# Moving the queries' second task one place ahead, and the first image's sums between its weight copies

## The chip, the core and the metric

The kernel runs on one core of a Trainium2 chip. The core has a matrix engine (TensorE, "PE"; its weight loads have a row of their own, "PEld"), an elementwise engine (VectorE, "DVE"), an engine for functions and copies (ScalarE, "ACT"), GpSimd ("POOL") and a queue that issues transfers ("SP"). Each engine works through its own list of instructions in order and waits at semaphores for the others. The metric is the device time in microseconds (us), as the median of several runs. One more run is recorded by the hardware profiler: that is the profile and the trace.

## The reference

Two layers of attention work on an image batch x of 8 x 32 x 32 x 256, in fp32. An image is N = 1024 rows of C = 256 values.

```
layer 0:  q, k, v = x W_qkv        4 heads, each 256 wide
          a = softmax(q k^T / 16)  over all 1024 rows of the image
          x1 = concat(a v) W_out + b_out + x
layer 1:  f = x1 Wf + bf;  g = x1 Wg + bg       32 wide
          h = x1 Wh + bh                        256 wide
          out = gamma * softmax(g f^T) h + x1
```

## The kernel before

**Folded weights.** Each head's matrices are folded once: wqk from the query and key weights, wvo from the value and output weights. Scores then need one projection of x (the "queries" q) against x itself, and the attention sums x rows directly, followed by one product with wvo. `fold_weights(h)` (L281) makes five tasks: three turns (transposes of the query, key and value weights on TensorE, each with a copy out of the accumulation memory) and two multiplications with their copies. `copy_on` puts copies on VectorE and ScalarE in turn. After wqk is copied, four sums of its quarters are made on VectorE (wt).

**Seven products instead of eight.** Layer 0's large products are cut in 2 x 2 blocks and done with seven block products (`seven`, L222). They need sums of blocks of both factors, made on VectorE: xs of the keys (`key_sums`, L346), xt of the values (`value_sums`, L362), qs of the queries and s/ss of the probabilities. A call of `seven` gives three tasks. It holds three banks of accumulation memory, x, y and z, throughout:

```
one:    x <- product 1, y <- 6, z <- 5;  e = copy of x (ScalarE);  u = y + e (VectorE)
two:    x <- x + 2, y <- y + 7;          11 = x (ScalarE);  v = y + e;  22 = z + v (VectorE)
three:  y <- y + 4, z <- z + 3;          21 = y + e;  12 = z + u (VectorE)
```

So TensorE's product 7 waits until u is made, and product 4 until v is made, since both add to a bank that VectorE reads. The instructions of all these tasks stand at one line of the profile, L235 for the matmuls and L252 for the additions, and are told apart by the tiles: psx_q, psy_q, psz_q, u_q, v_q belong to the queries, psx, psy, psz, u, v to scores, psx_y and so on to the products with the values. The pool "ps" has six banks and "psm" two; layer 1's scores (ps_l) and products (pa_l) take single banks of "ps", turns, folds and projections (po) those of "psm" (L762).

**Stages.** A unit is a head of layer 0 or an image's layer 1; a step is one half (blk 0 or 1, 512 columns) of a unit. An image's four heads are followed by the next image's; layer 1 of image b-1 stands behind the second head of image b (for the last image behind the fourth). The order on TensorE, VectorE and ScalarE is written out by hand: in each step i the tasks are put at places, numbers from about 0 to 10, and run in their order (`put`, L809). A step does the scores of its own unit, the sums and products of the step before (`one`), the rest of the products and the projection with wvo of the step before that (`two`), and in blk 1, if the next unit is a head, that head's queries (L841) and their sums qsums (L842). These are the places that a layer-0 step gives:

```
scores             0, 2, 4, 6, 8, 10     (two calls of seven, three tasks each)
products of two    1 (third task);  inverse 2.9;  projection 3 and 7
sums of one        2.2, 3.2, 4.2, 5.2;  products of one 5, 9
queries            1.5, 3.5, 4.5;  value_sums (h = 0, blk = 1, b > 0) 1.4, 2.4, 3.4, 4.4
```

A layer-1 step in blk 1 has its two tasks of four score matmuls (ps_l, each on 32 rows of the array, each followed by a copy to s_l on ScalarE) at 0.5 and 2, its softmax pieces from 0.9 to 7.5, the products of its first half (pa_l) at 1, 4, 6, 8, the projection at 3 and 7, and the queries at 2.5, 4.5 and 6.5.

**Start.** Ahead of step 0 come the transposes of the first image (px), the fold of head 0, the key sums, the first queries and their sums, the scaling of bh by gamma and the first image's value sums (L789 to L793). Step 0 then has the folds of heads 1 to 3, fifteen tasks at 0.3, 0.9, 1.5 and so on (L837).

Of the kernel before, what the change touches and what calls it, by code (L numbers as in the profile page):

```python
# [12 lines left out]
ALU = mybir.AluOpType  # L13
# [7 lines left out]
def kernel(  # L21
# [51 lines left out]
    nc = tc.nc  # L73
# [39 lines left out]
    rows, rows1 = {}, {}  # L113
# [36 lines left out]
    bh_sb = const.tile([P, C], F32, tag="bh", name="bh_sb")  # L150
    gamma_sb = const.tile([P, 1], F32, tag="gamma", name="gamma_sb")
# [129 lines left out]
    def fold_weights(h):  # L281

        wT, hold = [], []
        folded[h] = []

        def turn(i, what):
            w, _ = weights[h]
            pt = tile_of("psm", [P, NB], f"pw{what}_{h}")
            for d in range(CC):
                for c in range(CC):  # L290
                    nc.tensor.transpose(
                        pt[:, d * C + c * P : d * C + (c + 1) * P],
                        w[:, c, i * C + d * P : i * C + (d + 1) * P],
                        ident,
                    )
            if i != 1:
                hold.append(tile_of("y", [P, N], f"w{what}T_{h}"))
            t = hold[-1][:, ts(i % 2, NB)]
            copy_on(i, t, pt)
            wT.append(t.rearrange("p (d c) -> p d c", d=CC))  # L300

        def multiply(i, what):
            wqT, wkT, wvT = wT
            pm = tile_of("psm", [P, NB], f"p{what}_{h}")
            for c in range(CC):
                for d in range(CC):
                    nc.tensor.matmul(
                        pm[:, ts(c, C)],
                        lhsT=(wqT, wvT)[i][:, d, ts(c, P)],
                        rhs=wkT[:, d, :] if i == 0 else weights[h][1][:, d, :],  # L310
                        start=(d == 0),
                        stop=(d == CC - 1),
                    )
            t = const.tile([P, CC, C], F32, tag=f"{what}{h}", name=f"{what}{h}")
            copy_on(i, t.rearrange("p c e -> p (c e)"), pm)
            folded[h].append(t)
            if i == 0:
                t4 = const.tile([P, 4, P], F32, tag=f"wt{h}", name=f"wt{h}")
                sums = [t4[:, k, :] for k in range(4)]
                blocks = [t[:, c, ts(e, P)] for c in range(CC) for e in range(CC)]  # L320
                run(sum_b(sums, *blocks))
                wblocks[h] = b_operands(blocks, sums)

        tasks = [partial(turn, i, what) for i, what in enumerate(("q", "k", "v"))]
        tasks += [partial(multiply, i, what) for i, what in enumerate(("wqk", "wvo"))]
        return tasks


    xT_of, x1T_of, xblocks, vblocks = {}, {}, {}, {}

    def transpose_rows(b, src, dst, layer):


        def task(k, c):
            if b not in dst:
                dst[b] = tile_of("xT", [P, CC, N], f"x{layer}T_{b}")
            pt = tile_of("psm", [P, NB], f"px{layer}_{b}_{k}_{c}")
            for t in range(HT):
                nc.tensor.transpose(
                    pt[:, ts(t, P)], src[b][:, k * HT + t, ts(c, P)], ident  # L340
                )
            nc.scalar.copy(dst[b][:, c, ts(k, NB)], pt)

        return [partial(task, k, c) for k in range(NBLK) for c in range(CC)]

    def key_sums(b):  # L346

        made = {}

        def piece(i):  # L350
            if i == 0:
                xT = xT_of[b]
                t = tile_of("v", [P, 4, HN], f"xs_{b}")
                sums = [t[:, k, :] for k in range(4)]
                blocks = [xT[:, c, ts(k, HN)] for k in range(2) for c in range(CC)]
                made["l"] = sum_a(sums, *blocks)
                xblocks[b] = a_operands(blocks, sums)
            made["l"][i]()

        return [partial(piece, i) for i in range(4)]  # L360

    def value_sums(b):  # L362

        made = {}

        def piece(i):
            if i == 0:
                r = rows[b]
                t = tile_of("xt", [P, 4, NT // 2, P], f"xt_{b}")
                blocks = [r[:, ts(j, NT // 2), ts(c, P)] for j in range(2) for c in range(CC)]  # L370
                sums = [t[:, k] for k in range(4)]
                made["l"] = sum_b(sums, *blocks)
                vblocks[b] = b_operands(blocks, sums)
            made["l"][i]()

        return [partial(piece, i) for i in range(4)]
# [368 lines left out]
    def run(*lists):  # L745
        for l in lists:
            for t in l:
                t()
# [39 lines left out]

    first = steps[0][0]  # L789
    queries, qsums = first.queries()  # L790
    run(transpose_rows(0, rows, xT_of, 0), fold_weights(0), key_sums(0), queries, qsums)
    nc.vector.tensor_scalar(bh_sb, bh_sb, gamma_sb, None, ALU.mult)
    run(value_sums(0))  # L793

    def is_l0(s):
        return s is not None and isinstance(s[0], Layer0)
# [7 lines left out]
    for i, (a, blk) in enumerate(steps):  # L804
        l0 = isinstance(a, Layer0)
        one, two, nxt = step(i - 1), step(i - 2), step(i + 1)
        places = []

        def put(tasks, *at):  # L809
            assert len(tasks) == len(at)  # L810
            places.extend(zip(at, range(len(places), len(places) + len(at)), tasks))

        if l0:
            put(a.scores(blk), 0, 2, 4, 6, 8, 10)
        else:
            tasks, pieces = a.scores(blk)
            put(tasks, *((0.5, 2.4) if blk == 0 else (0.5, 2)))
            put(pieces, *((1.6, 3.9, 6.2, 6.5, 7.4, 8.4, 8.6) if blk == 0 else
                          (0.9, 2.7, 4.2, 5, 6.2, 6.8, 7.5)))
        if is_l0(two):  # L820
            u, k = two
            put(u.products_of[k][2:], 1 if l0 else 0)
            put([partial(u.invert, k)], 2.9 if l0 or blk == 1 else 1.9)
            put(u.project(k), *((3, 7) if l0 else (2, 6) if blk == 0 else (3, 7)))
        if is_l0(one):
            u, k = one
            sums, keys = u.sums(k)
            u.products_of[k] = u.products(k)
            put(sums[:2] + sums[3:], *((2.2, 3.2, 4.2) if l0 else (0.8, 2.2, 4.5)))
            put(sums[2:3], 5.2 if l0 else 5.5)  # L830
            put(keys, *((6.2, 8.2) if l0 else (7.6, 9.6)))
            put(u.products_of[k][:2], *((5, 9) if l0 else (4, 7)))
        elif one is not None:
            put(one[0].products(one[1]), *((3, 5, 7, 9) if l0 else (1, 4, 6, 8)))
        if i == 0:
            fold = fold_weights(1) + fold_weights(2) + fold_weights(3)
            put(fold, *[0.3 + 0.6 * n for n in range(len(fold))])  # L837

        if is_l0(nxt) and blk == NBLK - 1:
            queries, qsums = nxt[0].queries()  # L840
            put(queries, *((1.5, 3.5, 4.5) if l0 else (2.5, 4.5, 6.5)))  # L841
            put(qsums, *((5.4, 6.4, 7.2, 7.4) if l0 else (6.7, 6.9, 7.3, 7.6)))  # L842

        if l0 and a.h == 0 and blk == 0:
            put(residual(a.b), 5.3, 6.3, 7.3, 7.4)
        if l0 and a.h == 0 and blk == 1 and a.b > 0:
            put(value_sums(a.b), 1.4, 2.4, 3.4, 4.4)
        if l0 and a.h == 2 and blk == 0 and a.b + 1 < B:
            load_x(a.b + 1)
        if l0 and a.h == HEADS - 1 and blk == 0 and a.b + 1 < B:  # L850
            put(transpose_rows(a.b + 1, rows, xT_of, 0), 1.5, 2.5, 3.5, 4.5)
            put(key_sums(a.b + 1), 5.4, 6.4, 7.2, 7.4)

        if l0 and a.b > 0 and a.h == behind(a.b) - 1:
            if blk == 0:
                put(transpose_rows(a.b - 1, rows1, x1T_of, 1), 2.5, 4.5, 6.5, 8.5)
            else:
                put(nxt[0].queries(), 1.4, 1.5, 3.5)
        if not l0 and blk == 0:
            put(a.values(), 0.9, 1, 3, 5, 8)  # L860
        if nxt is None:
            put(transpose_rows(B - 1, rows1, x1T_of, 1), 8.1, 8.2, 8.3, 8.4)
            put(final.queries(), 9, 9.1, 9.3)
        for _, _, t in sorted(places, key=lambda x: x[:2]):
            t()
# [82 lines left out]
    with tc.If(bad > 0), ExitStack() as general:  # L948
# [5 lines left out]
        for b in range(B):  # L954
# [3 lines left out]
            for h in range(HEADS):  # L958
                a = General0(b, h)
# [4 lines left out]
            a = Layer1(b)  # L964
# [37 lines left out]
```

## Time and profile before

The time is 2407.64 us, the median of 3 runs (2407.25 to 2407.84). The profiled execution has a span of 2406.9 us.

| engine | busy us | share |
|---|---|---|
| TensorE, matmul | 2367.2 | 98% |
| TensorE, weight load | 1946.1 | 81% |
| VectorE | 1585.7 | 66% |
| ScalarE | 623.8 | 26% |
| GpSimd | 236.5 | 10% |

A row of the trace in order of time gives the start in us, how long it took, the engine, the line in the code, the operation, written tile<-read tiles, shapes and the number of instructions merged; brackets show how long the engine stood idle before it and whom it waited for. A row of the list of waits gives the waiting engine with the tile it wanted to write, the engine and tile that released it, and the total time, the number of times and the longest. Matmuls overlap a little: a row's duration is longer than the distance to the next row's start, and it is that distance which adds up to the span. A row of the view by stages gives the stage, its length, the busy time of each engine (with the number of instructions), the granted share of TensorE's clock, the share of the transfer engines and GB/s.

### The profile page before, as it was taken

What the parts mean: (1) busy time and instruction counts of PE and PEld (TensorE: products, weight loads), DVE (VectorE), ACT (ScalarE), POOL (GpSimd) and SP (SyncE); (2) the same over time, 40 slices, a digit from 0 to 9 for tenths busy, and PEclk for the clock granted to TensorE, in tenths of its full rate; (3) what the DMA queues carried; (4) which work ended last, traced back from release to release, by engine and by line L of the source; (5) the groups of instructions that cost most, each with busy time, mean ns of one, the idle gap of its engine ahead of it and who ended that gap; (6) DMA issues with size and microseconds to landing.
All of it is one profiled execution on the core that took longest, in us unless ns stands there. A gap on an engine that the chain in (4) does not pass through costs nothing.

```text
span 2406.9 us, 25909 instructions
## 1 busy us (share of the span) xinstructions
PE 2367.2 (98%) x10608; PEld 1946.1 (81%) x10608; DVE 1585.7 (66%) x2477; ACT 623.8 (26%) x1001; POOL 236.5 (10%) x93
## 2 busy tenths in 40 slices
PE   8999999999999999999999999999999999999999
PEld 6888888788887888778887788878888788888877
DVE  5666666567675666766667567675676756766665
ACT  2222222222232222322123222232222322222232
POOL 0111101011110111101111011110111100011110
PEclk9999999999999999999999999999999999999999
DMA  3000000000000000000000000000000000000000
GB/s 116 1 1 1 1 18 1 18 1 1 18 1 18 1 18 1 1 18 1 18 1 1 18 1 18 1 1 18 1 18 1 1 18 1 1 1 1 1 10 28
DMA packets 43535, 23.63 MB, mean 10 GB/s; under 512 B 36048, under 2 KB 38096, under 8 KB 43408
## 3 DMA queue, kind: packets, MB, share of 16 engines
q1 hardware_dynamic: 43408, 21.90, 3.2%
q8 instruction: 85, 1.39, 0.2%
q14 instruction: 42, 0.34, 0.0%
HBM read 13.37 MB, written 8.52 MB: 9 GB/s over the span
## 4 chain that ended last, share of the span: by engine, by line
PE 91%; DVE 8%; issue 0%; DMA 0%; ACT 0%; SPq 0%; DVEq 0%
PE psy_y L235 13%; PE psy L235 13%; PE pa_l L730 9%; PE psx_y L235 9%; PE psx L235 9%; PE psz_y L235 9%; PE psz L235 8%; PE po L586 8%; PE psy_q L235 3%; PE psz_q L235 2%; PE pr_v_l L419 2%; PE psx_q L235 1%; DVE s L529 1%; DVE ss L529 1%; PE pm_fg L399 1%; PE ps_l L651 1%
## 5 line engine op out<-in xcount | busy, mean ns | idle before, releaser
L542 POOL PARTITION_ALL_REDUCE rb<-rs x64 | 206.9, 3233 | 1942.2 <-DVE rs L540 1942.2
L235 PE MATMUL psy<-qs,xs 128*128 128x256 f32 x1024 | 262.9, 379 | 2.2 <-DVE qs L461 2.2
L235 PE MATMUL psz<-q,xs 128*128 128x256 f32 x1024 | 263.2, 380 | 0.0
L235 PE MATMUL psx<-q,x0T 128*128 128x256 f32 x1024 | 262.8, 379 | 0.0
L490 ACT ACTIVATE p<-p 128x1024 f32<-128x1024 f32 x128 | 135.4, 1058 | 456.9 <-DVE p L252 456.9
L586 PE MATMUL po<-wvo,y 128*128 128x256 f32 x1024 | 242.1, 379 | 0.0
L235 PE MATMUL psx_y<-p,x 128*128 128x256 f32 x1024 | 241.9, 379 | 0.0
L235 PE MATMUL psy_y<-s,xt 128*128 128x256 f32 x1024 | 241.9, 379 | 0.0
L730 PE MATMUL pa_l<-v_l,s_l 128*128 128x257 f32 x1024 | 231.7, 381 | 2.3 <-DVE y L252 1.9
L235 PEld LDWEIGHTS psx<-q,x0T 128*128 128x128 f32 x1024 | 193.9, 190 | 40.1 <-issue 15.8
L730 PEld LDWEIGHTS pa_l<-v_l,s_l 128*128 128x128 f32 x1024 | 193.7, 190 | 39.0 <-issue 12.7
L235 PEld LDWEIGHTS psx_y<-p,x 128*128 128x128 f32 x1024 | 192.9, 190 | 36.0 <-issue 12.0
L586 PEld LDWEIGHTS po<-wvo,y 128*128 128x128 f32 x1024 | 192.8, 190 | 31.2 <-issue 6.5
L235 PEld LDWEIGHTS psy<-qs,xs 128*128 128x128 f32 x1024 | 194.5, 190 | 29.0 <-DVE qs L461 2.6
L235 PEld LDWEIGHTS psz<-q,xs 128*128 128x128 f32 x1024 | 194.7, 190 | 26.5
L235 PEld LDWEIGHTS psy_y<-s,xt 128*128 128x128 f32 x1024 | 193.7, 190 | 27.3
L252 DVE TENSOR_TENSOR u<-psy,e 128x512 f32<-128x512 f32 x128 | 88.5, 692 | 164.3 <-PE psy L235 91.6
L264 ACT ACTIVATE p<-psx 128x512 f32<-128x512 f32 x128 | 76.4, 597 | 373.5 <-PE psx L235 373.4
L252 DVE TENSOR_TENSOR v<-psy,e 128x512 f32<-128x512 f32 x128 | 88.2, 689 | 115.1 <-PE psy L235 114.9
L235 PE MATMUL psy<-qs,x0T 128*128 128x256 f32 x512 | 131.4, 379 | 0.0
L258 ACT COPY e<-psx 128x512 f32<-128x512 f32 x128 | 73.9, 577 | 217.8 <-PE psx L235 217.8
L597 DVE SCALAR_TENSOR_TENSOR x<-po,inverse,x 128x256 f32<-128x256 f32 x256 | 112.0, 479 | 25.4 <-PE po L586 15.6
(108 smaller groups left out, 3152.6 us busy)
## 6 DMA issues: line engine op xcount, KB each, us to landing
out_dram<-x SPq DMA_DIRECT2D x15, 512.0 KB, 2.6
x<-in_x_dram SPq DMA_DIRECT2D x14, 512.0 KB, 4.6
w<-in_L_conv_W_qkv_dram SPq DMA_DIRECT2D x4, 768.0 KB
x<-in_x_dram SPq DMA_DIRECT2D x4, 256.0 KB, 4.7
w<-in_L_conv_W_out_dram SPq DMA_DIRECT2D x4, 256.0 KB, 9.8
line<-rb SPq DMA_DIRECT2D x64, 2.0 KB
st<-line SPq DMA_DIRECT2D x64, 2.0 KB, 2.1
out_dram<-x SPq DMA_DIRECT2D x4, 128.0 KB, 2.1
```

Of the source, the lines that this page charges most:

```text
L235: nc.tensor.matmul(banks[k][:, ts(i, w)], lhsT=lhsT, rhs=rhs, start=first and n == 0, stop=True, skip_group_check=True,)
L252: nc.vector.tensor_tensor(dst, shaped(banks[k]), shaped(other), ALU.add)
L258: nc.scalar.copy(scratch("e"), banks["x"])
L264: copy(outs["11"](), shaped(banks["x"]))
L399: nc.tensor.matmul(pm[:m], lhsT=w()[:, c, d * P : d * P + m], rhs=src()[:, c, ts(k, NB)], start=(c == 0), stop=(c == CC - 1),)
L419: nc.tensor.matmul(pm[:, ts(j, C)], lhsT=src()[:, c, ts(2 * t2 + j, P)], rhs=w()[:, c, :], start=(c == 0), stop=(c == CC - 1),)
L490: exp(both, both)
L529: made["l"][i]()
L542: nc.gpsimd.partition_all_reduce(t, r.rearrange("p e i -> p (e i)"), P, bass_isa.ReduceOp.add)
L586: nc.tensor.matmul(pm[:, ts(j, C)], lhsT=self.y[blk][:, c, ts(2 * t2 + j, P)], rhs=folded[self.h][1][:, c, :], start=(c == 0), stop=(c == ...
L597: nc.vector.scalar_tensor_tensor(acc, pm[:, ts(j, C)], inverse[:, n : n + 1], acc, ALU.mult, ALU.add)
L730: nc.tensor.matmul(pm[:, : C + 1], lhsT=p[:, j, ts(ti, P)], rhs=v[:, j, : C + 1], start=(j == 0), stop=(j == NT - 1),)
```

## The change

The queries' second task goes one place ahead, so that the projection and the scores' third task stand between it and the queries' third task. After a layer-1 unit and in step 1, where there is no projection, the first task goes ahead as well; inside a layer-1 unit all three do. At the start, three of the four key sums go between the copies of the folded weights, two turns of head 1 go ahead of the first scores, the other folds are spaced anew, and the first image's value sums and the scaling of bh move into step 1.

```
 queries, qsums = first.queries()
-run(transpose_rows(0, rows, xT_of, 0), fold_weights(0), key_sums(0), queries, qsums)
-nc.vector.tensor_scalar(bh_sb, bh_sb, gamma_sb, None, ALU.mult)
-run(value_sums(0))
+turn_q, turn_k, turn_v, *multiply = fold_weights(0)
+sums = key_sums(0)
+run(transpose_rows(0, rows, xT_of, 0), [turn_q, turn_k, sums[0], turn_v], sums[1:3])
+run(multiply, sums[3:], queries, qsums)
...
     fold = fold_weights(1) + fold_weights(2) + fold_weights(3)
-    put(fold, *[0.3 + 0.6 * n for n in range(len(fold))])
+    put(fold, -2, -1, *[0.9 + 0.6 * n for n in range(len(fold) - 2)])
+if i == 1:
+    put([partial(nc.vector.tensor_scalar, bh_sb, bh_sb, gamma_sb, None, ALU.mult)], 8.5)

 if is_l0(nxt) and blk == NBLK - 1:
     queries, qsums = nxt[0].queries()
-    put(queries, *((1.5, 3.5, 4.5) if l0 else (2.5, 4.5, 6.5)))
+    put(queries, *((1.5, 2.5, 4.5) if not l0 or is_l0(two) else (0.5, 1.5, 4.5)))
...
-if l0 and a.h == 0 and blk == 1 and a.b > 0:
+if l0 and a.h == 0 and blk == 1:
     put(value_sums(a.b), 1.4, 2.4, 3.4, 4.4)
```

## The prediction, made before the result was known

> **What bounds the kernel now.** I read the page first, then the list of waits, then TensorE's instructions in order of time around each gap. The page, busy time by engine:
>
> ```profile
> PE 2367.2 (98%) x10608; PEld 1946.1 (81%) x10608; DVE 1585.7 (66%) x2477; ACT 623.8 (26%) x1001; POOL 236.5 (10%) x93
> ```
>
> TensorE is busy 98% of 2406.9 us, so only what lies between its matmuls (39.7 us) can be won without removing matmuls, and the change removes none. The waits of TensorE name what ends those gaps (total us, times, longest):
>
> ```profile
> PE psy_q L235 <- DVE v_q L252: 21.5, 26, 1.5
> PE psy L235 <- DVE qs L461: 2.2, 1, 2.2
> PE psy_q L235 <- DVE xs L358: 0.7, 1, 0.7
> PE pwv L291 <- ACT wqT L172: 0.7, 1, 0.7
> ```
>
> The first is the third task of the queries waiting for VectorE's v_q, which must read bank y before TensorE adds to it. In order of time its 26 cases fall into three sizes plus the first, 0.78 at 22.56: 7 of 1.47 (steps with h=0, blk=1, b>0), 7 of 1.06 (i=1, and the L0 steps right after an L1 unit) and 11 of 0.27. One of the large ones:
>
> ```profile
> 607.00 1.02 PE L235 MATMUL psx_q<-x0T,wqk 128*128 128x512 f32 x2
> 607.86 1.02 PE L235 MATMUL psy_q<-xs,wt 128*128 128x512 f32 x2
> ...
> 608.81 0.88 DVE L597 SCALAR_TENSOR_TENSOR x<-po,inverse,x 128x256 f32<-128x256 f32 x2
> 609.58 1.03 PE L235 MATMUL psz<-q,xs 128*128 128x256 f32 x4
> 609.60 1.22 DVE L529 TENSOR_TENSOR s<-ss,p 128x1024 f32<-128x1024 f32 x1
> 610.74 0.69 DVE L374 TENSOR_TENSOR xt<-x,xt 128x512 f32<-128x512 f32 x1
> 611.34 0.69 DVE L252 TENSOR_TENSOR v_q<-psy_q,e_q 128x512 f32<-128x512 f32 x1
> 612.08 1.12 PE L235 MATMUL psy_q<-x0T,wt 128*128 128x512 f32 x2 [1.48 <-DVE v_q L252]
> 613.04 1.02 PE L235 MATMUL psz_q<-xs,wqk 128*128 128x512 f32 x2
> ```
>
> psy_q was done at 608.7, but v_q stands on VectorE behind two products, a sum and a value sum. Start to start a pair of matmuls takes 0.86; from 609.58 to 613.04 there should be 1.72 and are 3.46, so such a case costs 1.74. The same count gives 0.54 for a small case (126.80 to 129.06) and 1.32 for one after L1 (485.16 to 488.20). The six queries inside L1 units wait for nothing.
>
> At the start TensorE idles from 25.4 to 27.57, and its clock then falls to half:
>
> ```profile
> 25.60:28.90 3.30, 1.32 (x6) 1.20 (x7) 3.20 (x6) 0.43 (x1) 0.00 (x0) 1.00 0.34 138
> 28.90:32.40 3.50, 2.83 (x12) 2.11 (x10) 3.39 (x6) 0.58 (x1) 0.00 (x0) 0.51 0.00 0
> ```
>
> (The column before the last two is the granted clock, the third TensorE's busy time.)
>
> [...] four ps_l matmuls on 32 rows take 1.07 together (428.70 to 429.77). [...] The kernel gives 6 to "ps" and 2 to "psm", so a seventh live "ps" tile waits.
>
> **The change part by part.** I worked the times out by hand from the order and waits of the changed program and durations of these rows.
>
> *L0 steps behind an L0 unit, 18 cases.* The second task moves from behind the projection to ahead of it. TensorE then has two.queries, projection (1.72), three of scores (1.72), three.queries; VectorE has v_q before inverse, x and the second sum. In the case above: one.queries and two of scores end at 605.27 as before, two.queries at 606.99 (u_q done 603.65, no wait), projection to 608.71, scores to 610.44. VectorE: v 605.47, p, ss to 608.0, value sum to 608.6, v_q 608.6 to 609.2, the next add 609.9, both ahead of 610.44. No wait. VectorE then runs on without a gap: second sum to 612.2, value sum to 612.9; psy_y needs both and would start at 613.90. So 1.0 us of slack, and the whole 1.74 is kept: 7 x 1.74 = 12.2. The 11 small ones have 2.2 us of slack at the same place: 11 x 0.54 = 5.9.
>
> *L0 steps after an L1 unit and i=1, 7 cases.* Without a projection nothing lies between the tasks: the order is one.queries, two.queries, two of scores, three of scores, three.queries. The wait changes its tile: three of scores now follows two of scores at once and waits for v. Nearest row: the first queries, whose tasks also touch (20.75, 22.56, 23.52: 2.77 for 1.72, so 1.05 lost). 1.32 - 1.05 = 0.27, x 7 = 1.9 saved. In i=1 the first image's value sums (4 x 0.68 on VectorE) come in too; psy_y needs the third about 0.8 after it is there, so nothing.
>
> *L0 queries inside an L1 unit, 6 cases: a new wait.* Today all four ps_l of the second score task come before one.queries. Moved to 1.5 the queries hold three of six banks (x, y, z stay live until their third task) and ps_l gets three; in the changed program the fourth waits for ScalarE's copy of the first of the four. Rows:
>
> ```profile
> 428.70 1.14 PE L651 MATMUL ps_l<-fg 32*128 32x512 f32 x8
> 429.77 1.12 PE L235 MATMUL psx_q<-x0T,wqk 128*128 128x512 f32 x2
> 429.85 2.06 ACT L660 COPY s_l<-ps_l 128x512 f32<-128x512 f32 x4 [3.00 <-PE ps_l L651]
> 432.45 1.89 PE L586 MATMUL po<-wvo,y 128*128 128x256 f32 x8
> ```
>
> After: queries 428.70 to 431.27 (3 x 0.858); three ps_l at 431.27; copy of the first 1.15 later as in these rows, 432.43, taking 0.59 (median of the ps_l copies 596 ns), so 433.02; fourth ps_l at 433.07, alone 1.07; two.queries at 434.14 with 0.1 of restart, done 435.96. Before, the same work is done at 432.45 + 1.72 = 434.16. Loss 1.80, x 6 = 10.8. Queued behind the waiting ps_l: two.queries, projection, pa_l. VectorE's maximum, the all-reduce and s_l come some 4 us later; counted on, the third query sum ends about 451.8 and the next step's psy starts at 452.3, so no second wait, narrowly. Bounds: 0.9 if a lone ps_l overlaps what follows, 2.5 if that margin is gone.
>
> *Start.* Three key sums fit VectorE's gaps of 0.75 and 1.31 between copies (12.06 to 14.8), so psy_q starts at 17.21 rather than 18.08, and with the restart everything comes 0.96 earlier; no copy is delayed. Two turns of head 1 (0.86) fill the idle stretch while query sums run: saved. The idle stretch falls from 2.0 to about 1.3; waits of 1.48 in the 7 large cases never lowered the clock (whole rest of the span at 1.00), so I take it that the half clock goes: from 28.54 to 34.68 there are 6.14 us for 3.87 of matmuls, 0.8 of them the wait for wqT, 1.45 the clock. The wait for wqT goes too (0.8). The packed copies cost about 0.3 more waits than today's 0.24 and 0.35: fold tiles have two banks and each waits for a copy of 0.6 to 0.7. 0.96 + 0.86 + 1.45 + 0.8 - 0.3 = 3.8; bounds 2.3 (half clock stays) and 4.2.
>
> *At nothing:* bh times gamma (0.35, VectorE, late in i=1, used by the first L1 unit), the value sums leaving the start.
>
> Sum: 12.2 + 5.9 + 1.9 + 3.8 - 10.8 = 13.0. 2407.6 - 13.0 = **2394.6**.
>
> **The rivals.** *A, the L1 wait is hidden:* 2394.6 - 10.8 = 2383.8. For: three strips stand free while ps_l waits. Against: the next matmul needs all 128 rows and stands behind it. *B, VectorE binds in the h=0 steps:* from 605.5 to 616.9 it hardly rests, so the gap moves from v_q to psy_y and only 0.5 of 1.74 is kept (-8.7), and the half clock stays (-1.5): 2404.8. Against: the 1.0 of slack. *C, slower:* the h=0 steps keep nothing (-12.2), the half clock stays (-1.5), and L1 costs 3.0 (late softmax chain, then query sums: -7.2): 2394.6 + 20.9 = 2415.5. For: no wait stood there, margins are narrow. Against: all of it must go wrong.
>
> **How the numbers follow.** Forecast 0.72, A 0.08, B 0.10, C 0.10. Range: L1 bounds -5.4 and +4.2, the start -0.4 and +1.5, down to 2388.5; above I take in B, 2405; A and C (0.18) are left out. Faster by over 0.2% means under 2402.8: forecast, A and a little of B, 0.83; same 0.08; slower 0.09.
>
> **What would show it.** Right: psy_q waits for v_q of about 0.8 once instead of 21.5; psy waits for v, 7 times 0.8; ps_l waits for s_l on ScalarE, 6 times 0.7; no half clock near 29; psx of i=1 at about 52.6 instead of 56.46. Wrong: psy_y or psy waiting for xt, s2 or qs; ps_l without a wait; over 2.5 us lost per L1 unit.

## The result and the profile after

The changed kernel takes 2400.87 us (median of 6 runs, 2397.25 to 2401.66) against 2407.86 for the kernel before on the same chip: ratio 0.9967, 95% interval 0.9954 to 0.998, some 7 us less. Forecast were 13.0 us less, 2394.6. The time lies in the range, but almost half of the gain is missing, and the six runs spread over 4.4 us.

First line of the page after, busy time by engine:

```profile
PE 2373.5 (99%) x10608; PEld 1951.4 (81%) x10608; DVE 1584.2 (66%) x2477; ACT 623.7 (26%) x1001; POOL 236.5 (10%) x93
```

The span is 2399.1. What TensorE does not spend busy fell from 39.7 to 25.6 us, 14.1 less: more than forecast. But its busy time *rose* by 6.3 us (2367.2 before) with the same 10608 matmuls. So what is missing is not idle time; matmuls got slower somewhere. TensorE's waits first:

```profile
PE psy L235 <- DVE v L252: 5.5, 7, 0.8
PE px L339 <- DMA x<-in_x_dram: 4.9, 2, 4.0
PE ps_l L651 <- ACT s_l L660: 4.0, 6, 0.7
PE pa_l L730 <- DVE y L252: 1.9, 7, 0.3
PE psy L235 <- DVE qs L461: 1.3, 1, 1.3
PE psy_q L235 <- DVE v_q L252: 0.8, 1, 0.8
```

The 21.5 us of psy_q behind v_q are down to the first queries' 0.8. In their place stand seven waits of psy for v and six of ps_l for s_l, each with the number and size that were forecast. Here is one L1 unit in order of time, with the fourth ps_l behind its copy, and below it another unit whose order is the same:

```profile
423.22 1.02 PE L235 MATMUL psz_q<-xs,wt 128*128 128x512 f32 x2
424.17 1.13 PE L651 MATMUL ps_l<-fg 32*128 32x512 f32 x6
425.97 1.12 PE L651 MATMUL ps_l<-fg 32*128 32x512 f32 x2 [0.66 <-ACT s_l L660]
427.02 1.93 PE L235 MATMUL psx_q<-x0T,wqk 128*128 128x512 f32 x2
428.74 1.91 PE L235 MATMUL psy_q<-xs,wt 128*128 128x512 f32 x2
430.44 1.77 PE L586 MATMUL po<-wvo,y 128*128 128x256 f32 x7
...
722.51 1.12 PE L651 MATMUL ps_l<-fg 32*128 32x512 f32 x2 [0.66 <-ACT s_l L660]
723.56 1.12 PE L235 MATMUL psx_q<-x0T,wqk 128*128 128x512 f32 x2
724.52 1.02 PE L235 MATMUL psy_q<-xs,wt 128*128 128x512 f32 x2
725.38 1.89 PE L586 MATMUL po<-wvo,y 128*128 128x256 f32 x8
```

The two matmul pairs of psx_q and psy_q take 3.42 us from start to start in the first unit (427.02 to 430.44) and 1.82 in the second (723.56 to 725.38). The view by stages shows why (the column third from the end is the granted clock):

```profile
423.80:427.21 3.41, 2.75 (x11) 0.79 (x10) 0.38 (x1) 1.65 (x4) 0.00 (x0) 1.00 0.02 5
427.21:430.62 3.41, 3.41 (x5) 1.35 (x5) 0.00 (x0) 1.08 (x2) 0.00 (x0) 0.50 0.00 0
720.76:724.17 3.41, 2.75 (x11) 0.92 (x11) 0.00 (x0) 2.07 (x4) 0.00 (x0) 1.00 0.00 0
724.17:727.58 3.41, 3.41 (x15) 2.43 (x14) 1.97 (x3) 0.67 (x2) 0.00 (x0) 1.00 0.00 0
```

After the first unit's wait the clock is halved for 3.41 us. That happens in three of the six L1 units of this execution (from 427.2, 1608.2 and 1905.2). The distances between the steps' first psx in the two traces then give the whole account:

| steps | number | forecast each | measured each | sum measured |
|---|---|---|---|---|
| start, to the first psx of step 1 | 1 | -3.8 | -3.46 | -3.5 |
| L0 after L0, h = 0 | 7 | -1.74 | -1.74 | -12.2 |
| L0 after L0, others | 11 | -0.54 | -0.54 | -5.9 |
| L0 after L1, and step 1 | 7 | -0.27 | -0.27 | -1.9 |
| L1, clock stays full | 3 | +1.80 | +1.77 | +5.3 |
| L1, clock halved | 3 | +1.80 | +3.47 | +10.4 |

The sum is -7.8, which is 2399.1 - 2406.9. A halved stretch costs 3.47 - 1.77 = 1.70 us. The runs' mean granted clocks go with their times: 0.999 at 2397.25, 0.998 at 2398.51, 0.997 at the other four, 2400.8 to 2401.66. That fits a spread that is mostly the number of halved stretches, but only the profiled execution shows the stretches themselves.

### The profile page after: what moved, and what is told of

It is laid out like the page before. It is cut to its first block, busy times and chain, and to the rows that moved or that the text cites. A ratio compares the mean times of both kernels' runs of the same rounds, so it can differ in the third digit from the quotient of the medians.

```text
span 2399.1 us, 25946 instructions
## 1 busy us (share of the span) xinstructions
PE 2373.5 (99%) x10608; PEld 1951.4 (81%) x10608; DVE 1584.2 (66%) x2477; ACT 623.7 (26%) x1001; POOL 236.5 (10%) x93
## 4 chain that ended last, share of the span: by engine, by line
PE 96%; DVE 3%; ACT 0%; DMA 0%; issue 0%; SPq 0%; DVEq 0%; ACTq 0%
PE psy L235 14%; PE psy_y L235 13%; PE po L586 9%; PE pa_l L730 9%; PE psx_y L235 9%; PE psz L235 9%; PE psx L235 9%; PE psz_y L235 9%; PE psy_q L235 4%; PE psx_q L235 2%; PE psz_q L235 2%; PE pr_v_l L419 2%; PE ps_l L651 1%; PE px L339 1%; PE pm_fg L399 1%; DVE s_l L712 1%
## 5 line engine op out<-in xcount | busy, mean ns | idle before, releaser
L235 PEld LDWEIGHTS psx<-q,x0T 128*128 128x128 f32 x1024 | 193.9, 190 | 39.7 <-issue 15.3
```

Source lines behind the costliest of these rows:

```text
L235: nc.tensor.matmul(banks[k][:, ts(i, w)], lhsT=lhsT, rhs=rhs, start=first and n == 0, stop=True, skip_group_check=True,)
```

## The experiments

My theory (A) was that the loss sits in the L1 steps alone, begins with a shortage of banks, and is made worse by a clock that falls behind the 32-row matmuls around the wait, whether or not there is idle time (this last part, a supposition, is called W below). Rivals: the clock falls from idle time as such or from the new order as a whole (B, I), or early queries hold up layer 1's softmax (C). These letters are not those of the prediction's rivals.

**L1 part undone** (`e1_l1_back`).

```
-put(queries, *((1.5, 2.5, 4.5) if not l0 or is_l0(two) else (0.5, 1.5, 4.5)))
+put(queries, *((2.5, 4.5, 6.5) if not l0 else
+               (1.5, 2.5, 4.5) if is_l0(two) else (0.5, 1.5, 4.5)))
```

> The changed kernel with one part undone: the six queries inside layer-1 units stand at their old places 2.5, 4.5, 6.5. Theory A (bank shortage: queries ahead of the second score task hold three of six banks, the fourth ps_l waits, and the stretch of 32-row matmuls around that wait brings the half clock on): no wait of ps_l for s_l, no half clock between the start and the end, and each layer-1 step is back to the time of before (1.77 us less than a step without half clock, 3.47 less than one with): with six layer-1 steps about 2384.9 us, and hardly any spread between executions. Theory B (the half clock comes from TensorE's idle time in general, or from the new order as a whole): half-clock stretches stay, and the time is about 2390.

Measured: 2386.2 us (2385.22 to 2387.0), ratio 0.9908 (0.9892 to 0.9925). Its two longest waits of TensorE:

```profile
PE psy L235 <- DVE v L252: 5.5, 7, 0.8
PE px L339 <- DMA x<-in_x_dram: 5.0, 3, 3.6
```

No ps_l in the list, no halved clock between 14 us and the end (mean granted clock 1.0; 0.997 in the changed kernel), L1 steps as long as before. Theory A holds, B falls: all other moves together are free of the loss.

**L1 part alone** (`e2_l1_only`).

```
-put(queries, *((1.5, 3.5, 4.5) if l0 else (2.5, 4.5, 6.5)))
+put(queries, *((1.5, 3.5, 4.5) if l0 else (1.5, 2.5, 4.5)))
```

> The kernel before with one part of the change alone: the queries inside layer-1 units at 1.5, 2.5, 4.5. Theory A: the six waits of ps_l for s_l (0.66 each) come up here too, 6 x 1.77 = 10.6 us at full clock, and half-clock stretches in some of the six, 1.70 each: 2418 to 2429 us, differing from execution to execution. Theory B (the layer-1 move is harmless by itself and only harms together with the other moves): within 3 us of 2407.9.

Measured: 2421.28 us (2417.94 to 2421.69), ratio 1.0049 (1.0032 to 1.0066), 12.9 us slower.

```profile
PE psy_q L235 <- DVE v_q L252: 21.5, 26, 1.5
PE px L339 <- DMA x<-in_x_dram: 5.6, 2, 3.6
PE ps_l L651 <- ACT s_l L660: 4.0, 6, 0.7
```

The six waits are there with nothing else changed, and each of the six steps is 1.78 us longer, 10.7 in all. In the profiled execution none of them halved the clock (mean granted clock 0.999), as against three in the changed kernel (0.997); the other 2.0 of this trace's 12.7 us come before step 1, where the clock rose to full only at 15.9 us (11.9 in the trace of before). The times of the four runs do not follow their mean clocks here: three with 0.997 to 0.999 lie within 0.6 us.

**L0 after L0 alone** (`e3_l0_only`).

```
-put(queries, *((1.5, 3.5, 4.5) if l0 else (2.5, 4.5, 6.5)))
+put(queries, *(((1.5, 2.5, 4.5) if is_l0(two) else (1.5, 3.5, 4.5)) if l0
+               else (2.5, 4.5, 6.5)))
```

> The kernel before with one part alone: the second task at 2.5 in the 18 layer-0 steps that follow a layer-0 unit. If the terms of the prediction are right (7 x 1.74 + 11 x 0.54 = 18.1): 2389.8 us, the seven waits of 1.47 and the eleven of 0.27 gone, the seven of 1.06 left. If VectorE binds in the steps with value sums: about 2398, with psy_y waiting for VectorE.

Measured: 2390.76 us (2390.02 to 2393.2), ratio 0.993 (0.9913 to 0.9946), 17.6 less. The trace has seven steps shorter by 1.74 and eleven by 0.54, to the hundredth. VectorE does not bind; rival B of the prediction falls.

**The start alone** (`e4_start_only`): the changed kernel with the queries' places of before.

> The kernel before with one part alone: the new start (key sums between the weight copies, two turns ahead of the first scores, value sums and bh in step 1). Prediction: 3.8 us gained, 2404.1. The landmarks of the changed kernel's trace say 3.5, of which 0.4 came from a transfer that landed earlier: 2404.8. [...]

Measured: 2407.12 us (2406.21 to 2409.66), ratio 0.9996 (0.9987 to 1.0004): hardly anything. In its trace step 1 begins 3.10 us earlier than in that of before and ends only 0.37 earlier. The wait in step 1 before, and then step 1 of this kernel:

```profile
68.02 1.13 PE L235 MATMUL psy_q<-x0T,wt 128*128 128x512 f32 x2 [1.06 <-DVE v_q L252]
...
62.92 0.68 DVE L374 TENSOR_TENSOR xt<-x 128x512 f32<-128x512 f32 x1
63.52 1.22 DVE L529 TENSOR_TENSOR s<-ss,p 128x1024 f32<-128x1024 f32 x1
64.66 0.68 DVE L374 TENSOR_TENSOR xt<-x,xt 128x512 f32<-128x512 f32 x1
65.26 0.68 DVE L252 TENSOR_TENSOR v_q<-psy_q,e_q 128x512 f32<-128x512 f32 x1
66.00 2.07 PE L235 MATMUL psy_q<-x0T,wt 128*128 128x512 f32 x2 [2.13 <-DVE v_q L252]
67.86 1.77 PE L235 MATMUL psz_q<-xs,wqk 128*128 128x512 f32 x2
```

The value sums xt that the new start puts into step 1 stand ahead of v_q, the wait there grows from 1.06 to 2.13, and the clock is halved behind it (psy_q takes 2.07 rather than 1.13). The two parts of the change are not independent: with the queries at their old places, the new start loses in step 1 most of what it wins ahead of it. The twelve runs fall into two groups, seven at 2406.2 to 2407.1 and five, the profiled one among them, at 2408.8 to 2409.7 with a mean clock of 0.999 (six of the seven had 1.000). That fits a halved stretch which comes in some executions only, so the median holds some luck.

**The start and the queries of step 1** (`e8_start_step1`): as the last, with `(0.5, 1.5, 4.5) if i == 1`.

> The start of the changed kernel and the queries of step 1 alone at 0.5, 1.5, 4.5; everything else as before. The new start alone won 3.1 to 3.9 us by step 1 and lost 2.73 in step 1, where the value sums delay v_q at the old places (wait 2.1 and a half clock). If that is so: 3.5 + 0.3 us less than before, 2404.5. If value sums in step 1 cost by themselves: about 2407.

Measured: 2405.54 us (2404.43 to 2406.56), ratio 0.9986 (0.9979 to 0.9993), 2.7 less by the medians (the interval of the ratio is 1.7 to 5.1); in the trace step 1 is 0.27 us shorter than before. With v_q ahead of them the value sums are hidden.

**Layer 1's queries early, with a bank to spare** (`e6_l1_two`): the changed kernel, L1 places `(1.5, 1.9, 4.5)`.

> The changed kernel with the queries inside layer-1 units at 1.5, 1.9, 4.5: the second task too stands ahead of the second four score matmuls. Its copy frees bank x, so four banks are there for the four ps_l. Theory A (bank shortage): no wait of ps_l, no half clock, about 2386 us, though the queries are just as early as in the changed kernel. Theory C (early queries as such hold up ScalarE's and VectorE's softmax of layer 1): the six steps stay at about 1.8 us over those of before, 2397 us.

Measured: 2385.77 us (2385.65 to 2386.84), ratio 0.9904 (0.9888 to 0.9921), no wait of ps_l, no halved clock (mean granted clock 1.0). The first task is as early as in the changed kernel, but the second has given bank x back by the time ps_l asks for a fourth. Theory C falls; it is the bank.

**A quarter of the array, without idle time** (`e7_one_strip`): the kernel before; in eight places four ps_l run one after the other on one strip of 32 rows.

```
+k = 0 if blk == 1 and j0 > 0 else r
-lhsT=self.f[ts(r, CK), ts(j0 + r, P)], rhs=self.g[ts(r, CK), ts(blk, NB)]
+lhsT=self.f[ts(k, CK), ts(j0 + r, P)], rhs=self.g[ts(k, CK), ts(blk, NB)]
```

> The kernel before, and in the second score task of blk 1 of each of the eight layer-1 units the four ps_l matmuls all on the first strip of 32 rows (the same values lie in all four), so that they run one after the other: about 3.4 us of a quarter of the array without an idle moment, 2.4 us more in each of eight places, 19 us in all. Theory W [...]: half clock behind most of the eight, in all 8 x 1.7 = up to 14 us more, 2430 to 2441 us. Theory I (idle time alone): no half clock but near 29 us and at the end, about 2427.

Measured: 2440.96 us, one run. One of the places in order of time:

```profile
428.93 4.44 PE L652 MATMUL ps_l<-fg 32*128 32x512 f32 x8
433.31 2.08 PE L235 MATMUL psx_q<-x0T,wqk 128*128 128x512 f32 x2
435.17 1.91 PE L235 MATMUL psy_q<-xs,wt 128*128 128x512 f32 x2
436.88 1.87 PE L235 MATMUL psz_q<-xs,wt 128*128 128x512 f32 x2
438.59 1.89 PE L586 MATMUL po<-wvo,y 128*128 128x256 f32 x8
```

There is no gap, and yet the queries after it run at half clock. The clock falls already in the midst of the ps_l, after a stretch in which TensorE was busy throughout, in the view by stages:

```profile
428.34:431.75 3.41, 3.41 (x11) 1.59 (x10) 0.67 (x3) 1.17 (x2) 0.00 (x0) 1.00 0.08 1
431.75:435.17 3.42, 3.42 (x5) 0.89 (x4) 0.00 (x0) 1.17 (x2) 0.00 (x0) 0.50 0.02 5
```

It falls at six of the eight places, twice as long in this first one. Where it stays full a step is 2.55 us longer, where it is halved once 4.25: again 1.70. For comparison, one of the waits of 1.48 in the kernel before, with the stretch after it, both at full clock:

```profile
609.24:612.65 3.41, 1.94 (x9) 1.16 (x7) 3.38 (x6) 0.00 (x0) 0.00 (x0) 1.00 0.00 0
612.65:616.06 3.41, 3.41 (x15) 2.47 (x13) 3.41 (x6) 1.81 (x3) 0.00 (x0) 1.00 0.00 0
```

So 3.41 us with 1.94 busy, all with 128-row matmuls, kept the clock here; 3.41 us with 2.75 busy, about 2.2 of them with ps_l on one to three strips, were followed by half clock in three of the changed kernel's six L1 units; the four ps_l on one strip were, without idle time, in six of eight places. Half clock behind most of the eight and 2430 to 2441 us is what W had forecast, and I falls. Why the clock fell after these matmuls was not shown.

**The version that the experiments point to** (`e5_both`): L1 undone, and in the seven steps without a projection the queries' second task put between the scores' second and third, which touched each other.

```
+put(queries, *((2.5, 4.5, 6.5) if not l0 else
+               (1.5, 2.5, 4.5) if is_l0(two) else (1.5, 2.1, 4.5)))
```

> The changed kernel with two edits: queries inside layer-1 units back at 2.5, 4.5, 6.5, and in the seven layer-0 steps without a projection the tasks at 1.5, 2.1, 4.5, so that the second queries' task, and not nothing, stands between the scores' second and third task. If a wait after L1 is only a matter of one task of 1.72 us lying between (v needs about 1.1 us from the start of the last matmuls): psy no longer waits for v, 7 x 1.05 = 7.4 us less than the kernel with the layer-1 queries alone put back, about 2379 us. If VectorE is too late there (sums stand close behind): psy_q waits for v_q again, and the time stays near 2386.

Measured: 2378.5 us (2377.87 to 2378.76), ratio 0.9874 (0.9858 to 0.9891), 29.8 less than before and the least of all. A step after L1 in its trace:

```profile
473.25 1.03 PE L235 MATMUL psy<-qs,xs 128*128 128x256 f32 x4
474.12 1.02 PE L235 MATMUL psx_q<-x0T,wqk 128*128 128x512 f32 x2
474.32 0.69 DVE L252 TENSOR_TENSOR v<-psy,e 128x512 f32<-128x512 f32 x1 [1.84 <-PE psy L235]
474.97 1.02 PE L235 MATMUL psy_q<-xs,wt 128*128 128x512 f32 x2
475.83 1.03 PE L235 MATMUL psy<-qs,x0T 128*128 128x256 f32 x4
476.03 0.69 DVE L252 TENSOR_TENSOR v_q<-psy_q,e_q 128x512 f32<-128x512 f32 x1 [0.30 <-PE psy_q L235]
476.69 1.03 PE L235 MATMUL psz<-q,xs 128*128 128x256 f32 x4
477.56 1.02 PE L235 MATMUL psy_q<-x0T,wt 128*128 128x512 f32 x2
```

v is done at 475.0, before psy adds at 475.83; v_q at 476.7, before psy_q adds at 477.56. TensorE doesn't wait, and these steps are 1.33 us shorter than before, 1.05 more than in the changed kernel.

## Why the prediction was right, and where it was short

*Right, each by a part on its own:* the 18 steps behind an L0 unit (e3: 1.74 and 0.54); the wait that changes its tile after L1 (0.27, seven times 0.78 for v); VectorE's slack in the steps with value sums, where v_q ends at 604.8, ahead of psy_q at 606.00, and the value sum at 608.3, 1.1 us ahead of psy_y at 609.44 in the trace after (forecast 1.0); the shortage of banks in L1, whose cost at full clock is 1.77 (forecast 1.80), with no second wait behind it.

*Short:* the term "Loss 1.80, x 6". It counted the wait, the lone ps_l and the restart, all at full clock; what the clock might do was put at nothing there, without a reason. Measured in the profiled execution were 3 x 1.77 + 3 x 3.47, on average 2.62 a step, beyond the upper bound of 2.5, which I had drawn for another reason (late query sums) that did not come. The only reasoning on the clock, at the start, was that waits of 1.48 had never lowered it. It did not carry over: those waits stood among 128-row matmuls, and the clock stayed at 1.00; the new wait of 0.66 stands among 32-row ones, and 0.50 followed in three of six. That the time still lay in the range is in part luck: with all six stretches halved it would have been about 2406.0 (an estimate, 3 x 1.70 more), above the range's 2405. (The range's lower end, too, is 2388.8 by its own terms and not 2388.5.) Term by term, 13.0 forecast less 5.1 (three halved stretches), plus 0.2 (the L1 steps at full clock), less 0.3 (the start) is 7.8.

*The start* came out at 3.46 for 3.8, in part by luck, since two executions are compared whose clocks differ. The clock rose to full at 14.2 us, in the trace of before at 11.9, and the stretch from pwq to psx_q took 7.01 us for 6.10. The new order is not the cause: e5, with the same start and the rise at 12.0, took 6.13. With rises that lie close together, step 1 begins 3.92 us earlier (before and e5). The half clock near 29 us is gone, as forecast, and none of the six traces with the new start has it. But of the four with the old start only three have it: e3 does not, and its step 0 is 1.29 us shorter for that (forecast 1.45). Against e3, whose clock rose at 13.7, the changed kernel wins only 2.82. So the start is worth 2.8 to 3.9, by whether the old one would have had its half clock. e8 gives 2.7 for this part with step 1's 0.27, by the medians. That the start needs step 1's new order was not seen beforehand; in the change the two come together, so it cost nothing there.

*The rivals:* A (L1 hidden) is refuted by e2; B and C of the prediction by e3, since the h = 0 steps kept all of it. That L1 costs more was C's one true part.

*Left open:* which of the L1 stretches halve the clock. All six of the changed kernel have the same order and the same wait of 0.66, and the two shown above were both busy for 2.75 of 3.41 us, yet one was followed by 0.50 and the other by 1.00; in the trace of e2 all six kept full clock. No run was made to tell them apart.

## What to carry to other kernels

Where a task reads a bank that the next one adds to, put one other task of TensorE between them: in e5 1.7 us of matmuls hid what had cost 1.05. Before moving an accumulating group ahead, count the banks it holds for its whole life against what the tasks in between ask for at once, since a move that removes waits in one kind of step can make one in another. And apply a new order only in the steps that had the wait; six that had none gave back 15.7 of the 20.0 us that the other 25 won.

## What the runs showed of the hardware

In e7 the TensorE clock fell to 0.50 without idle time: TensorE was busy for the whole of the 3.41 us ahead (428.34 to 431.75), the last 2.8 of them with 32-row matmuls on one strip. It fell at six of the eight places, for 3.41 us or twice that, and one halved stretch of 3.41 us made a step 1.70 us longer (4.25 for 2.55). In the changed kernel it fell behind three of six waits of 0.66 among such matmuls, at the same 1.70 (3.47 for 1.77). Among 128-row matmuls, 3.41 us with 1.94 busy were followed by full clock (before, from 609.24), while behind the wait of 2.13 in e4 the clock was halved (a pair in 2.07 us for 1.13). The clock's first rise to full came at 11.9 to 16.2 us in the ten traces, and the time of the start moved with it: with the same new start, the stretch from pwq to psx_q took 6.13 us where the clock rose at 12.0 (e5), 7.01 where it rose at 14.2 (the changed kernel) and 7.91 where it rose at 16.2 (e8).
